# Two layers of cross attention: a lower place in the order for VectorE's transposes, and output products held back at the end

## The chip, the cores and the metric

The kernel runs on one core of one Trainium2 chip. The metric is the device time of one execution, in microseconds (us). A core has five engines that run their own instruction streams and wait for each other by semaphores: PE (TensorE, matrix products; its weight loads are listed apart as PEld), DVE (VectorE), ACT (ScalarE), POOL (GpSimd) and SP, which here only issues DMA transfers.

## The reference

Everything is float32: x is 8 x 100 x 512, the context 8 x 361 x 512. A first layer is a cross attention without heads. Then come two cross attentions with 16 heads of 128, and an MLP. Cut to what matters:

```python
def _cross_attention(q_in, kv_in, wq, bq, wk, bk, wv, bv, wo, bo, bias_k, bias_v):
    qh = (q_in @ wq + bq).reshape(b, q_len, H, K)          # H = 16, K = 128
    kh = (kv_in @ wk + bk).reshape(b, t, H, K)             # and one bias key
    vh = (kv_in @ wv + bv).reshape(b, t, H, K)             # and one bias value
    logits = jnp.einsum('bqhk,bthk->bhqt', qh, kh) / scale
    weights = jax.nn.softmax(logits, axis=-1)
    ctx = jnp.einsum('bhqt,bthk->bqhk', weights, vh).reshape(b, q_len, H * K)
    return ctx @ wo + bo
...
    x = x + alpha * (softmax(q k / sqrt(512)) v) @ w_o.T    # first layer, no heads
    x = x + _cross_attention(layer_norm(x), ctx, ...)       # twice, own weights
    x = x + gelu(layer_norm(x) @ w_fc1 + b_fc1) @ w_fc2 + b_fc2
```

## The kernel before, in words

**Steps.** The keys and values are never formed. Queries are multiplied by wq (pq, L623) and then by the head's key weights (pqw, L639, into the large buffer Z), and the scores are the product with the context itself. In the same way the softmax weights are first mixed with the context (into Z), and the value weights come after, in the output product. The eight batches go in four pairs (q = 0 to 3), and the 16 heads in three groups (g = 0, 1, 2) whose 100-row heads lie one after the other as 1600 rows: rows 0 to 576, 576 to 1088 and 1088 to 1600. So there are 24 steps (l, q, g) for the two layers l, and each has two halves j, one for each batch of the pair.

**One half.** Rows are taken in pairs of 128 (L692). A pair's scores are seven block products of a Strassen-Winograd scheme (PE L680/683, tiles sx, sy, sz), put together by copies on ACT (L708, L711, L714, L728) and additions on DVE (L718, L723, L724). The sums of blocks that it needs are made on POOL (L666 to L669), and POOL also writes the bias key's column (L717). Then: maximum on DVE (L736), exponential on ACT (L737), reciprocal (L313) and scaling (L314), and `turned` (L323), which turns the rows into columns by DVE transposes of 32 x 32 blocks (L329): four quarters of four instructions for a pair, written into the tile pT. When the last quarter of a group's last pair is done, `column_sums` (L752) sends the bias column to DRAM (L756, on SP's queue) and makes four sums on POOL (L757 to L760).

**Mix.** `mixed` (L784) multiplies pT with the context, again by a scheme of seven products, for two column halves m and in four parts each. Part 0 starts the tiles mx and mz (mz uses M1, which reads the result of L757); part 1 uses M2, which reads that of L759; part 2 makes M3 in mx and the tile my; part 3 makes A22 and A23 in the same PSUM bank as mx. Between part 2 and part 3 DVE has to read mx:

```python
            add(x, M3, 1)
            ...
            nc.vector.tensor_tensor(c22, x, c22, ALU.add)     # L819
            nc.vector.tensor_tensor(c11, y, c11, ALU.add)     # L820
        else:
            add(x, A22, 8, last=False)
```

L793 is the matmul in `add`; evictions go to ACT (L802, L805, L810, L824) and DVE (L813, L819, L820).

**Output.** `bias_probs` (L828) fetches the bias column's probabilities for a group, in two DMAs on SP's queue into the one buffer pb. `head_out` (L836) makes a head's output product: one POOL operation (L842), eight passes on PE (po, L845) against the weights wv, and one DVE operation (L852) into the tile oT. The weights wv come in a ring of two slots. `attn_out` (L863, pwo L869) is the product with wo for a batch pair, 128 passes, and `back` (L872) turns the result and adds it to x. The MLP consists of the norm's transposes (ph L540, then DVE L543), `hidden` (L883, pg L893) and `mlp_out` (L898, pf L905). L543 and ph are used for the query projections too.

**The order.** The program is a list of units. The main loop (from L1016) takes a half's score units in groups and lays the filling between them: the closing of the pair before (`close_units`), the projections of the next step (`ahead`), the mix of the half before, and, in halves j=1, the output products of the step before. `woven` spreads one list over another. `lead` is how many of the filling units come before the mix. After the loop comes `drain`: the last mix, output products and closing, with the MLP's norm between them. What the list says is not yet each engine's order: a scheduler takes instructions by priority, which is their place in the program, as they become ready by its own reckoning. `tc.high_priority(offset=-30)` around a block gives its instructions the priority of a place 30 later. Loads of weights go on SP's queue in the order of their use, as their ring's slots come free. P buffers (probabilities) are three, tiles of `sums` two, and all products share eight PSUM banks.

Of the kernel before, what the change touches and what calls it, by code (L numbers as in the profile page):

```python
# [16 lines left out]
B, L, S, D = 8, 100, 361, 512  # L17
# [5 lines left out]
QB = 2  # L23
# [10 lines left out]
WHOLE = ((0, 5), (5, 10), (10, 16))  # L34
# [8 lines left out]
A11, A12, A22, A13, A23, A33, M1, M2, M3, M4 = range(10)  # L43
LN_EPS = 1e-5
W_SLOTS, V_SLOTS, C_SLOTS, P_SLOTS = 6, 2, 2, 3
QD = 32


# [30 lines left out]
def two_cross_attentions(ctx: ExitStack, tc: tile.TileContext, a: dict, out: bass.AP):  # L79
    nc = tc.nc  # L80
# [11 lines left out]
    def psum(pool, shape, name):  # L92
        return pool.tile(shape, F32, tag=pool.name, name=name)
# [91 lines left out]
    units = []  # L185

    def unit(fn, *keys):
        return fn, keys
# [26 lines left out]
    for c in range(DT):  # L215
        rows = slice(c * P, (c + 1) * P)
# [106 lines left out]
    def turned(p, dst, tiles, rows, quarter):  # L323

        keys = slice(quarter * QD, (quarter + 1) * QD)
        src = p[:, :tiles, :].rearrange("p m (k j b) -> p m k j b", k=3, b=QD)
        dst = dst.rearrange("p k (m i a) -> p m k i a", m=tiles, a=QD)
        for i in range(rows // QD):
            nc.vector.transpose(dst[keys, :, :, i, :], src[i * QD : (i + 1) * QD, :, :, quarter, :])  # L329

    def ln_stats(b):
        st = small.tile([L, 6], F32, tag="stats", name=f"stats_{b}")
# [451 lines left out]
    def mixed(l, q, g, j, m, part):  # L784
        cx = rings["ctx"].tiles["ctx", l, q * QB + j].rearrange("p (m u n) -> p m u n", m=2, n=P)[:, m]
        pT = pTs[l, q, g, j]
        r0, r1 = ROWS[g]
        h = (r1 - r0) // 2
        c11, c12 = Z[:, 2 * m, j, r0 : r0 + h], Z[:, 2 * m, j, r0 + h : r1]
        c21, c22 = Z[:, 2 * m + 1, j, r0 : r0 + h], Z[:, 2 * m + 1, j, r0 + h : r1]  # L790

        def add(ps, blk, u, first=False, more=True, last=True, w=P):
            nc.tensor.matmul(  # L793
                ps, cx[:w, blk, :], pT[:w, u, :], start=first, stop=last, skip_group_check=more
            )

        name = f"{l}_{q}_{g}_{j}_{m}"
        if part == 0:
            x, z = psum(ps_mm, [P, h], f"mx_{name}"), psum(ps_mm, [P, h], f"mz_{name}")
            mixes[m] = x, z  # L800
            add(x, A11, 0, True, False)
            nc.scalar.copy(c11, x)  # L802
            add(z, M1, 6, True, False, False)
            add(z, A23, 5, more=False, w=TS)
            nc.scalar.copy(c22, z)  # L805
            return
        x, z = mixes[m]
        if part == 1:
            add(x, M2, 7)
            nc.scalar.copy(c12, x)  # L810
            add(z, M4, 3, last=False)
            add(z, A33, 5, w=TS)
            nc.vector.tensor_tensor(c12, z, c12, ALU.add)  # L813
        elif part == 2:
            add(x, M3, 1)
            y = psum(ps_mm, [P, h], f"my_{name}")
            add(y, A12, 2, True, False, False)
            add(y, A13, 4, more=False, w=TS)
# [4 lines that stand above are left out]
            add(x, A23, 4, w=TS)  # L823
            nc.scalar.copy(c21, x)  # L824
# [3 lines left out]
    def bias_probs(l, q, g):  # L828
        h0, h1 = WHOLE[g]
        t = work.tile([P, QB, 600], F32, tag="pb", name=f"pb_{l}_{q}_{g}", bufs=1)  # L830
        for j in range(QB):
            src = pbd[l, q * QB + j].rearrange("o r -> (o r)")[h0 * L : h1 * L]
            nc.sync.dma_start(out=t[:, j, : (h1 - h0) * L], in_=src.partition_broadcast(P))
        pbs[l, q] = t, h0

    def head_out(l, q, h):  # L836
        if (l, q) not in oTs:
            oTs[l, q] = opool.tile([P, H, NQ], F32, tag="o", name=f"oT_{l}_{q}")
        w = rings["v"].tiles["wv", l, q, h // 2].rearrange("p (c n) -> p c n", c=DT)
        t, h0 = pbs[l, q]  # L840
        add = t[:, :, (h - h0) * L : (h - h0 + 1) * L]
        nc.gpsimd.tensor_scalar(add, add, dv[:, l, h : h + 1], 1.0, ALU.mult, ALU.mult)  # L842
        ps = psum(ps_mm, [P, NQ], f"po_{l}_{q}_{h}")
        for c in range(DT):
            nc.tensor.matmul(  # L845
                ps,
                w[:, c, (h % 2) * K : (h % 2 + 1) * K],
                Z[:, c, :, h * L : (h + 1) * L],
                start=(c == 0),
                stop=(c == DT - 1),  # L850
            )
        nc.vector.scalar_tensor_tensor(  # L852
            oTs[l, q][:, h, :].rearrange("p (b t) -> p b t", b=QB),
            ps.rearrange("p (b t) -> p b t", b=QB),
            vec[f"bv{l + 1}"][:, h : h + 1],
            add,
            ALU.add,
            ALU.add,
        )
# [3 lines left out]
    def attn_out(l, q, c):  # L863
        if c == 0:
            ys[l, q] = work.tile([P, DT, NQ], F32, tag="y", name=f"y_{l}_{q}", bufs=1)
        ps = psum(ps_mm, [P, NQ], f"pwo_{l}_{q}_{c}")
        for h in range(H):
            w = w8(("wo", l, q, c, h // 8))
            nc.tensor.matmul(ps, w[:, h % 8, :], oTs[l, q][:, h, :], start=(h == 0), stop=(h == H - 1))  # L869
        nc.scalar.activation(ys[l, q][:, c, :], ps, AF.Identity, bias=vec_b[:, 6 + l, c : c + 1])  # L870
# [42 lines left out]
    steps = [(l, q, g) for l in range(2) for q in range(B // QB) for g in range(NG)]  # L913
# [27 lines left out]
    def mix_units(n, j):  # L941
        l, q, g = steps[n]
        return [
            unit(lambda m=m, part=part: mixed(l, q, g, j, m, part), ("ctx", ("ctx", l, q * QB + j)))
            for m in range(2)
            for part in range(4)
        ]

    def out_units(n):
        l, q, g = steps[n]  # L950
        return [unit(lambda h=h: head_out(l, q, h), ("v", ("wv", l, q, h // 2))) for h in range(*WHOLE[g])]

    def close_units(l, q):
        res = [
            unit(lambda c=c: attn_out(l, q, c), (W, ("wo", l, q, c, 0)), (W, ("wo", l, q, c, 1)))
            for c in range(DT)
        ]
        res += [unit(lambda j=j: back(ys[l, q], j * L, q * QB + j, ln_stats)) for j in range(QB)]
        return res
# [9 lines left out]

    def woven(x, y):  # L970

        res, k = [], 0
        for n, u in enumerate(x):
            res.append(u)
            upto = (n + 1) * len(y) // len(x)
            res += y[k:upto]
            k = upto
        return res
# [37 lines left out]
    for n, (l, q, g) in enumerate(steps):  # L1016
        ahead = project_units(n + 1) if n + 1 < len(steps) else []
        half_ahead = (len(ahead) + 1) // 2
        for j in range(QB):
            fill = []  # L1020
            if j == 0 and n and g == 1 and (l, q) != (0, 0):
                pl, pq, _ = steps[n - 2]
                fill += close_units(pl, pq)
            mix = mix_units(n, 0) if j else mix_units(n - 1, 1) if n else []
            part = ahead[:half_ahead] if j == 0 else ahead[half_ahead:]
            if j and n:
                outs = [unit(lambda n=n: bias_probs(*steps[n - 1]))] + out_units(n - 1)
                part = woven(part, outs) if len(part) > len(outs) else woven(outs, part)
            if mix:
                lead = (len(part) + 2) // 3  # L1030
                fill += part[:lead]
                part = part[lead:]
                fill += woven(part, mix) if len(part) > len(mix) else woven(mix, part)
            else:
                fill += part
            if l == 0 and q == 1:
                k = 2 * g + j
                fill += e_units(1)[4 * k // 3 : 4 * (k + 1) // 3]
            groups = score_units(n, j)
            k = 0  # L1040
            for i, us in enumerate(groups):
                units += us
                upto = (i + 1) * len(fill) // len(groups)
                units += fill[k:upto]
                k = upto
    n = len(steps) - 1
    drain = mix_units(n, 1) + [unit(lambda: bias_probs(*steps[n]))] + out_units(n)
    drain += close_units(1, B // QB - 1)
    norm, hid, mlp, end = mlp_units(0)
    norm1, hid1, mlp1, end1 = mlp_units(1)  # L1050
    units += woven(drain, norm)
    units += hid + woven(mlp, norm1) + woven(hid1, end) + mlp1 + end1
    emit()

# [24 lines left out]
```

## Time and profile before

| | |
|---|---|
| three runs, us | 2100.14, 2094.68, 2097.88 (median 2097.88) |
| the profiled execution, us | 2100.8 |
| its span, us | 2099.0 |
| its mean granted TensorE clock | 0.993 |
| PE idle within the span, us | 76.6 |
| memory traffic | 256.87 MB, mean 122 GB/s |

The profile is one execution. A line of a timeline gives the start, the length, the engine, the line of the kernel, the operation, what it writes and reads, how many instructions it groups, and in brackets how long the engine stood before it and what ended that. In the list of groups, the two numbers after the first bar are busy time in us and the mean of one instruction in ns. In a list of windows, each row gives the window's length, the busy time of PE, PEld, DVE, ACT and POOL (with the number of instructions), the granted clock of TensorE (1.00 is full), the busy share of the DMA engines and GB/s.

The 24 steps take most of the span, about 71 us each. The stretch from 1892 us on is the last output projection and the MLP.

### The profile page before, as it was taken

The page shows a single profiled execution, that of the slowest core. Times are in us where ns is not written, and L with a number is a line of the kernel's source. Part 1 is how long each engine was busy: PE and PEld are TensorE (multiplying, and loading weights), DVE is VectorE, ACT ScalarE, POOL GpSimd, SP SyncE. Part 2 cuts the span into 40 slices and gives each one's busy share as a digit, 9 for nine tenths or more (in the row PEclk, how much of TensorE's full clock was granted, in tenths as well). Part 3 has the DMA queues.
Part 4 walks back from the last instruction along what each step waited for, and adds up shares of the span by engine and source line. Part 5 has one row for each costly group of instructions (what it writes and reads, how often), then busy time and mean ns, then how long its engine had stood idle before and what let it go on. Part 6 is the DMA issues. An engine that isn't in the chain of part 4 may idle for free. (4 is left out here: it accounts for less than half of the span.)

```text
span 2099.0 us, 30154 instructions
## 1 busy us (share of the span) xinstructions
PE 2022.4 (96%) x10735; PEld 1774.3 (85%) x10735; DVE 1159.0 (55%) x3363; ACT 749.0 (36%) x1962; POOL 572.1 (27%) x1042
## 2 busy tenths in 40 slices
PE   9998999999999999999999999999999999989998
PEld 5768899898899898989898999899998998877555
DVE  2564776657764666466645665475647574661000
ACT  1224544424342444234423443344324442421110
POOL 3232442333242224223331323232322322310000
PEclk9999999999999999999999999999999999999999
DMA  8784325342544133414442344224332434113331
GB/s 251 260 293 136 96 76 182 119 147 79 158 128 140 61 122 119 150 36 141 155 140 82 106 131 131 84 86 143 108 110 81 151 95 120 51 53 121 100 102 50
DMA packets 254109, 256.87 MB, mean 122 GB/s; under 512 B 35756, under 2 KB 226640, under 8 KB 250632
## 3 DMA queue, kind: packets, MB, share of 16 engines
q1 hardware_dynamic: 249776, 244.58, 37.6%
q0 software_dynamic: 2112, 6.40, 0.9%
q10 hardware_dynamic: 2072, 3.97, 0.6%
q8 instruction: 85, 1.39, 0.3%
q14 instruction: 64, 0.52, 0.1%
HBM read 229.24 MB, written 25.67 MB: 121 GB/s over the span
## 5 line engine op out<-in xcount | busy, mean ns | idle before, releaser
L329 DVE STREAM_TRANSPOSE pT<-p 32x192 f32<-32x192 f32 (+1 forms) x1664 | 602.0, 362 | 85.4 <-ACT p L314 59.5
L793 PE MATMUL mx<-pT,ctx 128*128 128x256 f32 (+3 forms) x960 | 284.5, 395 | 32.7 <-DVE Z L819 28.6
L683 PE MATMUL sx<-cT,Z 128*128 128x181 f32 x1152 | 228.2, 317 | 5.0 <-DVE p L723 5.0
L793 PE MATMUL mz<-pT,ctx 105*128 105x256 f32 (+3 forms) x768 | 209.7, 395 | 13.9 <-POOL pT L757 12.3
L793 PEld LDWEIGHTS mx<-pT,ctx 128*128 128x128 f32 (+1 forms) x960 | 170.0, 190 | 55.7 <-DVE Z L819 31.2
L683 PEld LDWEIGHTS sx<-cT,Z 128*128 128x128 f32 x1152 | 195.2, 190 | 18.0 <-DVE p L723 6.5
L845 PE MATMUL po<-Z,wv 128*128 128x200 f32 x1024 | 199.0, 336 | 0.5 <-DMA wv<-in_L_xattn_wv_dram 0.5
L623 PE MATMUL pq<-hT,wq 128*128 128x200 f32 x1024 | 195.7, 335 | 3.9 <-DMA wq<-in_L_xattn_wq_dram 3.9
L639 PE MATMUL pqw<-q,wkT 128*128 128x200 f32 x1024 | 196.5, 334 | 0.0
L793 PEld LDWEIGHTS mz<-pT,ctx 128*128 128x128 f32 (+1 forms) x768 | 145.1, 192 | 49.6 <-POOL pT L757 16.3
L623 PEld LDWEIGHTS pq<-hT,wq 128*128 128x128 f32 x1024 | 176.6, 191 | 9.6 <-DMA wq<-in_L_xattn_wq_dram 4.1
L639 PEld LDWEIGHTS pqw<-q,wkT 128*128 128x128 f32 x1024 | 177.5, 191 | 5.4 <-issue 0.5
L845 PEld LDWEIGHTS po<-Z,wv 128*128 128x128 f32 x1024 | 176.5, 191 | 6.6 <-issue 1.6
L869 PE MATMUL pwo<-oT,wo 128*128 128x200 f32 x1024 | 176.0, 332 | 0.0
L869 PEld LDWEIGHTS pwo<-oT,wo 128*128 128x128 f32 x1024 | 173.3, 190 | 0.1
L737 ACT ACTIVATE p<-p,nm 128x362 f32<-128x362 f32 x192 | 114.8, 598 | 160.1 <-DVE nm L736 158.5
L666 POOL TENSOR_TENSOR sums<-Z 128x256 f32<-128x256 f32 x96 | 69.9, 728 | 348.7 <-ACT Z L642 194.1
L736 DVE TENSOR_REDUCE nm<-p 128x1 f32<-128x362 f32 x192 | 101.6, 529 | 98.2 <-ACT p L728 84.7
L642 ACT COPY Z<-pqw 128x400 f32<-128x400 f32 x256 | 122.9, 489 | 83.4 <-PE pqw L639 83.2
L683 PE MATMUL sz<-cT,sums 128*128 128x181 f32 x768 | 149.9, 317 | 0.0
L314 ACT ACTIVATE p<-p,rden 128x362 f32<-128x362 f32 (+2 forms) x216 | 129.6, 600 | 29.8 <-DVE rden L313 29.0
L683 PEld LDWEIGHTS sz<-cT,sums 128*128 128x128 f32 x768 | 124.5, 190 | 1.3 <-ACT p L711 1.3
(310 smaller groups left out, 2627.1 us busy)
## 6 DMA issues: line engine op xcount, KB each, us to landing
wv<-in_L_xattn_wv_dram SPq DMA_DIRECT2D x64, 512.0 KB
wq<-in_L_xattn_wq_dram SPq DMA_DIRECT2D x64, 512.0 KB
wo<-in_L_xattn_wo_dram SPq DMA_DIRECT2D x64, 512.0 KB
wkT<-wkd SPq DMA_DIRECT2D x48, 512.0 KB
cT<-cTd SPq DMA_DIRECT2D x16, 1267.0 KB
f<-in_L_xattn_w_fc_dram SPq DMA_DIRECT2D x32, 512.0 KB
wkr<-in_L_xattn_wk_dram SPq DMA_DIRECT2D x16, 512.0 KB
ctx<-cxd SPq DMA_DIRECT2D x16, 512.0 KB
```

What stands on the lines that cost most here:

```text
L314: nc.scalar.mul(p[:rows, :n], p[:rows, :n], rden[:rows])
L329: nc.vector.transpose(dst[keys, :, :, i, :], src[i * QD : (i + 1) * QD, :, :, quarter, :])
L623: nc.tensor.matmul(ps, w[:, c, (h % 2) * K : (h % 2 + 1) * K], hTs[l, q][:, c, :], start=(c == 0), stop=(c == DT - 1),)
L639: nc.tensor.matmul(ps[:, c, :], w[:, h % 2, cc * P : (cc + 1) * P], qs[h], start=True, stop=True)
L642: nc.scalar.copy(Z[:, 2 * c2 : 2 * c2 + 2, :, h * L : (h + 1) * L], ps.rearrange("p c (b t) -> p c b t", b=QB),)
L666: nc.gpsimd.tensor_tensor(t[:, 0], a2[:, :2, :], a2[:, 2:, :], ALU.add)
L683: nc.tensor.matmul(ps[:, :KH], st["a"][a][:, c, :], st["ct"][:, blk, c, :], start=(first and c == 0), stop=(c == 1), skip_group_check=not ...
L736: nc.vector.tensor_reduce(nm, p[:, :S1], AX.X, ALU.max, negate=True)
L737: nc.scalar.activation(p[:, :S1], p[:, :S1], AF.Exp, bias=nm, accum_out=den)
L793: nc.tensor.matmul(ps, cx[:w, blk, :], pT[:w, u, :], start=first, stop=last, skip_group_check=more)
L845: nc.tensor.matmul(ps, w[:, c, (h % 2) * K : (h % 2 + 1) * K], Z[:, c, :, h * L : (h + 1) * L], start=(c == 0), stop=(c == DT - 1),)
L869: nc.tensor.matmul(ps, w[:, h % 8, :], oTs[l, q][:, h, :], start=(h == 0), stop=(h == H - 1))
```

## The change

There are two parts.

First, the 16 transposes of a pair (and the eight of a first group's single tile of 64 rows) are issued with a priority 30 places later than where they stand. Nothing else about them changes.

Second, the output products are regrouped at the end. `out_units` now begins with the unit of `bias_probs`, which stood beside it before. In step 22 (the last but one), j=1, the output units of step 21 are not laid into the filling; they are put, with those of step 22, into `held`: twelve units, bias and heads 0 to 4, bias and heads 5 to 9. Step 23 takes six of them in its half j=0 and three (bias, heads 5 and 6) in j=1, where before it had those of step 22 in j=1. The last three (heads 7, 8, 9) come after the loop, followed by four of the eight transposes of the MLP's norm, and then the last mix and what follows it, with the other four. In step 23, `lead` is all but the last two of the filling units in j=0, and all but one in j=1. For all other steps the list of units stays as it was: `woven` now returns its second list when the first is empty, since a half with no output products passes through it too.

```diff
--- before.py
+++ after.py
@@ -43,6 +43,7 @@
 A11, A12, A22, A13, A23, A33, M1, M2, M3, M4 = range(10)
 LN_EPS = 1e-5
 W_SLOTS, V_SLOTS, C_SLOTS, P_SLOTS = 6, 2, 2, 3
+TURN_BEHIND = 30
 QD = 32
 
 
@@ -325,8 +326,9 @@
         keys = slice(quarter * QD, (quarter + 1) * QD)
         src = p[:, :tiles, :].rearrange("p m (k j b) -> p m k j b", k=3, b=QD)
         dst = dst.rearrange("p k (m i a) -> p m k i a", m=tiles, a=QD)
-        for i in range(rows // QD):
-            nc.vector.transpose(dst[keys, :, :, i, :], src[i * QD : (i + 1) * QD, :, :, quarter, :])
+        with tc.high_priority(offset=-TURN_BEHIND):
+            for i in range(rows // QD):
+                nc.vector.transpose(dst[keys, :, :, i, :], src[i * QD : (i + 1) * QD, :, :, quarter, :])
 
     def ln_stats(b):
         st = small.tile([L, 6], F32, tag="stats", name=f"stats_{b}")
@@ -948,7 +950,8 @@
 
     def out_units(n):
         l, q, g = steps[n]
-        return [unit(lambda h=h: head_out(l, q, h), ("v", ("wv", l, q, h // 2))) for h in range(*WHOLE[g])]
+        res = [unit(lambda h=h: head_out(l, q, h), ("v", ("wv", l, q, h // 2))) for h in range(*WHOLE[g])]
+        return [unit(lambda: bias_probs(l, q, g))] + res
 
     def close_units(l, q):
         res = [
@@ -969,6 +972,8 @@
 
     def woven(x, y):
 
+        if not x:
+            return y
         res, k = [], 0
         for n, u in enumerate(x):
             res.append(u)
@@ -1023,11 +1028,16 @@
                 fill += close_units(pl, pq)
             mix = mix_units(n, 0) if j else mix_units(n - 1, 1) if n else []
             part = ahead[:half_ahead] if j == 0 else ahead[half_ahead:]
-            if j and n:
-                outs = [unit(lambda n=n: bias_probs(*steps[n - 1]))] + out_units(n - 1)
-                part = woven(part, outs) if len(part) > len(outs) else woven(outs, part)
+            outs = []
+            if n == len(steps) - 1:
+                outs = held[:6] if j == 0 else held[6:9]
+            elif j and n:
+                outs = out_units(n - 1)
+                if n == len(steps) - 2:
+                    held, outs = outs + out_units(n), []
+            part = woven(part, outs) if len(part) > len(outs) else woven(outs, part)
             if mix:
-                lead = (len(part) + 2) // 3
+                lead = (len(part) + 2) // 3 if ahead else len(part) - 2 + j
                 fill += part[:lead]
                 part = part[lead:]
                 fill += woven(part, mix) if len(part) > len(mix) else woven(mix, part)
@@ -1044,11 +1054,10 @@
                 units += fill[k:upto]
                 k = upto
     n = len(steps) - 1
-    drain = mix_units(n, 1) + [unit(lambda: bias_probs(*steps[n]))] + out_units(n)
-    drain += close_units(1, B // QB - 1)
+    drain = mix_units(n, 1) + out_units(n) + close_units(1, B // QB - 1)
     norm, hid, mlp, end = mlp_units(0)
     norm1, hid1, mlp1, end1 = mlp_units(1)
-    units += woven(drain, norm)
+    units += held[9:] + norm[:4] + woven(drain, norm[4:])
     units += hid + woven(mlp, norm1) + woven(hid1, end) + mlp1 + end1
     emit()
 
```

The line numbers of the changed kernel are those of before plus one from L46 to L327, and plus two from L328 to L949: L819 becomes L821, L757 becomes L759.

## The prediction, made before the changed kernel was run

> **What bounds the kernel now.** I read the share of busy time first, then the engine's waits, then the timeline around the commonest wait, then ten-microsecond windows of the end.
>
> ```profile
> span 2099.0 us, 30154 instructions
> PE 2022.4 (96%) x10735; PEld 1774.3 (85%) x10735; DVE 1159.0 (55%) x3363; ACT 749.0 (36%) x1962; POOL 572.1 (27%) x1042
> ...
> L329 DVE STREAM_TRANSPOSE pT<-p 32x192 f32<-32x192 f32 (+1 forms) x1664 | 602.0, 362 | 85.4 <-ACT p L314 59.5
> ```
>
> PE is busy for all but 76.6 us of the span (2099.0 - 2022.4). The change adds no matmul, so it can win only from those 76.6 us and from time that PE is busy at a lower granted clock. The second engine, DVE, spends over half of its busy time in the transposes, 0.37 us each, in blocks of 16. PE's waits say what the 76.6 us are:
>
> ```profile
> engine line waited for: us in total, times, longest us
> PE mx L793 <- DVE Z L819: 28.6, 19, 2.1
> PE mz L793 <- POOL pT L757: 12.3, 8, 5.0
> PE sx L683 <- DVE p L723: 5.0, 3, 1.7
> PE pqk L350 <- DMA Z<-in_L_xattn_w_q_dram: 4.7, 1, 4.7
> PE sx L683 <- ACT p L708: 4.4, 5, 1.6
> ...
> PE mx L793 <- POOL pT L759: 2.7, 6, 0.5
> ```
>
> The first line is the largest. One of its places:
>
> ```profile
> 1560.81 6.11 DVE L329 STREAM_TRANSPOSE pT<-p 32x192 f32<-32x192 f32 x16 [0.66 <-ACT p L314]
> 1561.19 1.14 PE L793 MATMUL my<-pT,ctx 128*128 128x288 f32 x4
> 1566.96 0.46 DVE L819 TENSOR_TENSOR Z<-mx,Z 128x288 f32<-128x288 f32 x1
> 1567.01 0.73 POOL L757 TENSOR_TENSOR pT<-pT 128x256 f32<-128x256 f32 x1 [12.74 <-DVE pT L329]
> 1567.33 0.45 DVE L820 TENSOR_TENSOR Z<-my,Z 128x288 f32<-128x288 f32 x1
> 1567.47 1.24 PE L793 MATMUL mx<-pT,ctx 128*128 128x288 f32 x4 [1.88 <-DVE Z L819]
> ```
>
> The product M3 is in PSUM at about 1561.4, but DVE has 16 transposes ahead of the addition of L819, which starts at 1566.96. The last part of the mix writes the same PSUM bank as M3, so PE stands until L819 is done: 1.88 us. The transposes themselves have no such hurry here: the column sums they feed (L757 to L760) end near 1570, and the next mix reads them at 1573.58.
>
> The end of the attention has its own waits, all after 1790:
>
> ```profile
> 1817.20 1.13 PE L793 MATMUL mz<-pT,ctx 128*128 128x256 f32 x4 [1.99 <-POOL pT L757]
> 1831.52 0.88 PE L683 MATMUL sx<-cT,Z 128*128 128x181 f32 x4 [1.58 <-DVE p L723]
> 1842.46 1.13 PE L793 MATMUL mz<-pT,ctx 128*128 128x256 f32 x4 [2.37 <-POOL pT L757]
> 1869.88 2.08 PE L793 MATMUL mz<-pT,ctx 128*128 128x256 f32 x4 [4.97 <-POOL pT L757]
> ```
>
> No next step's projections are left there to fill PE, so the chain scores, softmax, transposes, column sums, mix stands open. After 1892 the output projection and MLP run without a gap.
>
> Some waits also cost afterwards: PE goes on at half clock for a while.
>
> ```profile
> 1783.00:1784.00 1.00, 1.00 (x4) 0.71 (x3) 0.00 (x0) 0.00 (x0) 0.92 (x3) 0.50 0.00 0
> 1860.00:1870.00 10.00, 5.03 (x27) 4.25 (x25) 8.12 (x22) 2.68 (x7) 0.81 (x2) 0.88 0.18 53
> ```
>
> The column after the engines is the granted clock: 0.50 after the 1.88 us wait at 1781.96. The same four matmuls took 2.02 us there and 1.24 us at 1567.47.
>
> **The skill.** "TensorE: Matmul & The Clock Gate", Part 1, says that TensorE falls to half clock after an idle window of about 3.4 us, that the window runs freely, and that this varies between runs. The trace agrees on the size of the drop (0.50, for some 3.4 us), not on the idle time: waits of 1.88 us already did it, though only at 911.4, 1351.7 and 1782.0 and not at 697, 1137 and 1567. "Perfetto Trace Analysis", GPSIMD and Tensor Engine sections, says that VectorE and GpSimd execute in strict order, which is what the 16 transposes ahead of L819 show. "VectorE: DVE Perf Modes", The three transpose paths, says the transpose works on 32x32 blocks; its price is for another type, so I use the trace's 0.37 us.
>
> **The change part by part.** The built program has the same number of instructions on every engine as before. Their static order tells what moved.
>
> *Transposes later, steps 0 to 21.* At places of the kind above (first head group, j=1, m=1), DVE had 16 transposes, L819, L820; it now has 3, L819, 2, L820, 11. At those of the third group (j=0, m=1) it had 15, L819, L820; it now has 5, L819, 2, L820, 4, L852, 4. L819 comes 10 to 13 transposes sooner, 3.7 to 4.8 us, against waits of 1.3 to 2.05 us. PE's own order changes too: the last mx part moves earlier at 13 places, ahead of an output product or other work that had covered part of DVE's delay. So the wait does not vanish by 3.7 us of slack: in the first group the part stands directly behind my, reached about 1562.2 in the example, and L819 would end about 1562.4; I leave 0.3 us at seven places, 2.1 us together, and none in the third group.
>
> Waits at the 13 places in the trace of before: 1.88, 1.89, 2.05, 1.88, 1.88, 1.88 (first group) and 1.88 (at 1083.88), six of 1.62 (third group): 13.3 + 9.7 = 23.1 us. Less 2.1: -21.0 us.
>
> What pays: the block's last transposes end later by what was put between them, 0.46 + 0.45 = 0.9 us in the first group, 1.25 with L852 in the third. The first has about 3.5 us of cover between the sums' end and the mix, the third at least 8: nothing. The second group's j=1 columns have none: at 1386.93 and its likes mz waits 0.3 us for L757 and mx then 0.54 for L759. One L543 (0.48 us) now precedes their last transpose: 6 places x 0.48 = 2.9 us. On POOL, L757 stands in most groups behind the pair of L717 (2 x 0.19 us). Where there is cover this is free, at those six places at most 2.3; I take 1.0, as L717 often waits for nothing. Sum of the body: -21.0 + 2.9 + 1.0 = about -17 us. Bounds: the additions nothing (-21), or twice what I take (-13).
>
> *Clock.* The drops at 911, 1352 and 1782 each cost half of 3.4 us, 1.7: 5.1 in all. Those waits go. The second group's waits become near 1.4 us together and could bring one drop back: -4 (bounds -5 and 0; a new wait of 1.9 would be as bad).
>
> *Held output products.* For step 22, bias and heads of steps 21 and 22 no longer stand before the last scores; six units go into step 23 j=0, three into j=1, heads 7 to 9 behind it with four transposes of the MLP's norm, then the last mix. Eight passes of L845 take 1.35 us, so some 13 us of PE work moves into or behind the open chain. But it is taken from before it: step 22 j=1 loses its filling, so its own waits, of some 0.2, open up. Stepping through PE, DVE, ACT and POOL in the new order with the durations of before, I get waits of 0.2, 1.3, 0.2, 0.5, 0.5, 1.4, 1.1, 0.5, 1.4, 0.5, 0.4, 4.1 and 0.55 (the wv load at 1888.73, moved with its ring of two slots): 12.6 us, where before has 1.99 + 1.58 + 0.28 + 2.37 + 4.97 + 0.55 = 11.7. The last wait stays, since its 16 transposes now share DVE with four L852 (1.7 us) while the held heads cover PE. Of the two half-clock stretches (1844 to 1847, 1867 to 1875, about 1.7 and 2.2 us) I expect one to go. +0.9 - 1.8: -1 us. Bounds: the steps lie on waits of a microsecond each, so -8 (the moved work covers the last two waits) to +5 (a late L757 behind L717, L667, L668 and L669 on POOL, 0.73 each for the last three, and another drop). On SP the bias loads and the wv loads come later with their heads, wo loads earlier; PE's pwo comes 20 us later, so nothing.
>
> Sum: -17 - 4 - 1 = -22 us. The profiled execution took 2100.8 us (span 2099.0 and 1.8 outside it): 2078.8. It stands 2.9 above the median of 2097.88, so on that scale 2076.
>
> **The rivals.** *Given back:* the wait on L819 goes, but PE, earlier by 1.9 us a step, meets the same DVE chain at the next use (scores at L723, columns at L757). For it: the waits on L723 and L708 already exist, 9.4 us. Against: DVE is at 55%, and the first and third groups have cover of microseconds. Half of the 22 stays: 2087 (2083 to 2095).
> *The end gains too:* held heads fill the 4.97 and 2.37 waits and both drops go: -8 instead of -1, and the additions in the body cost nothing (-4 more): 2065. For it: 13 us of PE work is moved there. Against: the step-through, in which DVE's 21.7 us in step 23 j=0 are the limit.
> *Column sums late (slower):* the transposes, 30 places lower, are overtaken by more than the order of the built program makes cheap: L757 on POOL waits behind L717, L667 to L669 for a score step that PE itself has put after the mix. Place: the mz that reads M1, 44 column sums in steps 0 to 21. It has to cost more than 23 + 6 us, so an average above 0.66 us of new wait at each of the 44; each long one may add 1.7 for the clock. At 0.9 us each with five drops: 40 + 8 - 23 = +25, less what the drops now cost (-5): about 2115. For it: L757 already makes the second line of the waits, and POOL holds four 0.73 us operations ahead. Against: 38 of the 44 have cover above the 0.9 to 1.3 us they get later.
> *Doesn't do what it says:* excluded, the static order shows the moved additions.
>
> **How the numbers follow.** Forecast 0.62 (2076, own range 2069 to 2084), given back 0.15, end too 0.10, late sums 0.13. The bound of what can be told is 0.3%, 6.3 us. Faster: 0.62 + 0.10 + two thirds of 0.15 = 0.82, take 0.81; same: 0.06; slower 0.13. The range 2063 to 2094 leaves out the slower case and edges of the others, about 0.18.
>
> **What would show it.** In the waits of the changed kernel: the line of L819 (now L821) falls from 28.6 to below 8 us with no place above 1.3 outside the end; L757 and L759 (L759, L761) grow by 3 to 5 us outside the end; PE's idle total falls to about 58 us; no clock of 0.8 in ten-microsecond windows around 911, 1352 and 1782. After 1790 the idle time stays near 12 us, with one wait of about 4 before the last mix. The prediction is wrong if L757's line grows past 25 us, if waits on L723 or L708 grow by the amount L819 loses, or if the end's idle falls below 5.

## The result, and the profile after

The changed kernel takes 2074.22 us (median of four runs, 2070.76 to 2074.61) against 2096.28 us before (median of four): a ratio of 0.9891, 95% interval 0.9869 to 0.9913. The profiled execution took 2074.07 us. Its page begins:

```profile
span 2072.3 us, 30186 instructions
...
PE 2014.7 (97%) x10735; PEld 1770.9 (85%) x10735; DVE 1165.6 (56%) x3363; ACT 748.5 (36%) x1962; POOL 575.7 (28%) x1042
```

PE idles 57.6 us (2072.3 - 2014.7) instead of 76.6, and is busy 7.7 us less with the same matmuls. Its waits (us in total, times, longest):

```profile
PE mz L795 <- POOL pT L759: 9.4, 7, 3.8
PE sx L685 <- ACT p L710: 6.7, 4, 3.1
PE mx L795 <- DVE Z L821: 5.5, 9, 1.9
PE mx L795 <- POOL pT L761: 5.2, 7, 1.4
...
PE sx L685 <- DVE p L725: 4.8, 5, 2.3
```

The line of L819 (now L821) falls from 28.6 to 5.5 us; the column sums' second line (L759, now L761) rises from 2.7 to 5.2. The timeline of the changed kernel at the place that the prediction took as its example:

```profile
1541.07 1.13 DVE L331 STREAM_TRANSPOSE pT<-p 32x192 f32<-32x192 f32 x3 [0.67 <-ACT p L315]
1541.45 1.14 PE L795 MATMUL my<-pT,ctx 128*128 128x288 f32 x4
1542.24 0.46 DVE L821 TENSOR_TENSOR Z<-mx,Z 128x288 f32<-128x288 f32 x1
1542.73 0.75 DVE L331 STREAM_TRANSPOSE pT<-p 32x192 f32<-32x192 f32 x2
1542.75 1.24 PE L795 MATMUL mx<-pT,ctx 128*128 128x288 f32 x4 [0.16 <-DVE Z L821]
1543.51 0.46 DVE L822 TENSOR_TENSOR Z<-my,Z 128x288 f32<-128x288 f32 x1
```

Three transposes instead of 16 stand ahead of the addition, and PE waits 0.16 us instead of 1.88. PE's own order changed with it, as predicted: the last part of mx now follows directly behind my, where before products of pqw, sx, sz and po stood between, which had covered some 3.4 us of DVE's delay. Now the place that pays, the second group's second half. First two lines of before, then the changed kernel:

```profile
1601.14 1.13 PE L793 MATMUL mz<-pT,ctx 128*128 128x256 f32 x4 [0.29 <-POOL pT L757]
1602.81 0.70 PE L793 MATMUL mx<-pT,ctx 128*128 128x256 f32 x2 [0.54 <-POOL pT L759]
```

```profile
1573.75 4.20 DVE L331 STREAM_TRANSPOSE pT<-p 32x192 f32<-32x192 f32 x11
1577.98 0.48 DVE L545 TENSOR_SCALAR hT<-ph,vec_b 128x200 f32<-128x200 f32 x1
1578.48 0.76 DVE L331 STREAM_TRANSPOSE pT<-p 32x192 f32<-32x192 f32 x2
1579.32 0.72 POOL L759 TENSOR_TENSOR pT<-pT 128x256 f32<-128x256 f32 x1 [0.91 <-DVE pT L331]
1580.10 1.13 PE L795 MATMUL mz<-pT,ctx 128*128 128x256 f32 x4 [0.82 <-POOL pT L759]
...
1582.15 0.70 PE L795 MATMUL mx<-pT,ctx 128*128 128x256 f32 x2 [0.92 <-POOL pT L761]
```

L545 (before: L543) has slipped in ahead of the last two transposes. The two waits are 0.82 and 0.92 us, where before they were 0.29 and 0.54, with one of 0.20 behind them (at 1604.01, on ACT).

To compare runs without the first part of the execution, which varies from run to run (the first mark below lies between 423.8 and 431.0 us in the traces of this study) and in which PE's idle time is nearly the same, 20.8 us before and 20.9 after, I take the first matmul of each of the eight `attn_out` (pwo) as a mark. "Steps" is the stretch from the first such mark to the next to last, "end" the one from there to the last. In before they are 428.79 to 1731.27 and 1731.27 to 1891.74. "Clock lost" is the length times one minus the granted clock, summed over windows of two microseconds; it counts also the half clock during which PE stands. A stretch of half clock lasts 3.4 us in these traces, or twice that, and so counts as 1.7 us or 3.4.

| | steps, us | PE idle | clock lost | end, us | PE idle | clock lost |
|---|---|---|---|---|---|---|
| before | 1302.5 | 35.5 | 3.4 | 160.5 | 13.7 | 6.8 |
| after | 1281.0 | 20.1 | 1.7 | 157.3 | 9.7 | 5.1 |

The steps give 21.5 us and the end 3.2. One interval without any half clock in either trace shows what a wait costs. The window views, before and then after (length, then busy time of PE, PEld, DVE, ACT and POOL, then the granted clock, here 1.00, DMA share and GB/s):

```profile
1516.79:1731.27 214.48, 209.53 (x1170) 194.23 (x1169) 130.97 (x366) 85.46 (x226) 64.03 (x118) 1.00 0.37 111
```

```profile
1497.05:1707.70 210.65, 208.55 (x1170) 194.35 (x1169) 131.28 (x366) 85.46 (x226) 64.42 (x118) 1.00 0.36 113
```

It is 3.83 us shorter, but only 2.85 of that is idle time (4.95 to 2.10). The other 0.98 is busy time for the same 1170 matmuls. The timeline shows six waits of 0.2 to 1.88 us in the first and three of 0.16 to 0.92 in the second, so some 0.3 us of busy time goes with each wait.

### The profile page after: what moved, and what is told of

The parts are those of the page before. It is cut to its first block, busy times and chain, and to the rows that moved or that the text cites. A ratio compares the mean times of both kernels' runs of the same rounds, so it can differ in the third digit from the quotient of the medians.

```text
span 2072.3 us, 30186 instructions
## 1 busy us (share of the span) xinstructions
PE 2014.7 (97%) x10735; PEld 1770.9 (85%) x10735; DVE 1165.6 (56%) x3363; ACT 748.5 (36%) x1962; POOL 575.7 (28%) x1042
## 5 line engine op out<-in xcount | busy, mean ns | idle before, releaser
L795 PE MATMUL mx<-pT,ctx 128*128 128x256 f32 (+3 forms) x960 | 282.7, 393 | 12.9 <-DVE Z L821 5.5
L847 PE MATMUL po<-Z,wv 128*128 128x200 f32 x1024 | 193.9, 333 | 0.6 <-DMA wv<-in_L_xattn_wv_dram 0.6
L719 POOL TENSOR_SCALAR p<-nsb 128x1 f32<-128x1 f32 x192 | 33.3, 193 | 526.3 <-DVE pT L331 481.8
```

Of the source, the lines that this page charges most:

```text
L795: nc.tensor.matmul(ps, cx[:w, blk, :], pT[:w, u, :], start=first, stop=last, skip_group_check=more)
L847: nc.tensor.matmul(ps, w[:, c, (h % 2) * K : (h % 2 + 1) * K], Z[:, c, :, h * L : (h + 1) * L], start=(c == 0), stop=(c == DT - 1),)
```

## The experiments

All ratios are to before, with 95% intervals, from five rounds each. They change only the order of the work.

**One part alone, twice.** The first run takes the transposes' priority alone:

```diff
+TURN_BEHIND = 30
...
+        with tc.high_priority(offset=-TURN_BEHIND):
+            for i in range(rows // QD):
+                nc.vector.transpose(dst[keys, :, :, i, :], src[i * QD : (i + 1) * QD, :, :, quarter, :])
```

> Only the transposes 30 places later; the output products of the last steps stay where they were before. Theory A (the gain is the wait on L819, at 13 places of the steps and the one near 1782; the held output products give nothing): 2074 to 2077 us, ratio to before 0.989 to 0.991; PE's line of waits for L819 near 6 us; the idle time behind 1760 near 12 us. Theory B (the held products give a third or more of the gain): 2081 to 2085 us, ratio 0.993 to 0.995.

The second takes all else of the change and leaves the transposes where they were:

```diff
-        with tc.high_priority(offset=-TURN_BEHIND):
-            for i in range(rows // QD):
-                nc.vector.transpose(dst[keys, :, :, i, :], src[i * QD : (i + 1) * QD, :, :, quarter, :])
+        for i in range(rows // QD):
+            nc.vector.transpose(dst[keys, :, :, i, :], src[i * QD : (i + 1) * QD, :, :, quarter, :])
```

> Only the output products held back; the transposes keep their priority. Theory A: 2095 to 2099 us, ratio 0.999 to 1.001, the wait on L819 at 28 us as before, and the idle time of the last steps moved from some places to others but not smaller than 11 us. Theory B: 2087 to 2091 us, ratio 0.995 to 0.997.

Measured: transposes alone 2076.69 us, 0.9903 (0.9883 to 0.9922); held products alone 2095.14 us, 0.9984 (0.9976 to 0.9993). Theory A holds for the first. For the second neither theory does: the time lies within A's range, but the ratio is below it and the idle time of the last steps below A's 11 us. The held products alone do gain, 0.16%, some 3 us, less than B asked. The trace shows a gain in the end, which is 156.4 us instead of 160.5, with 9.6 us of idle time instead of 13.7:

```profile
1731.04:1887.46 156.42, 146.81 (x778) 133.30 (x777) 90.84 (x251) 48.61 (x135) 40.85 (x74) 0.97 0.26 75
```

So I had the held products too small by themselves. Where the transposes are late, though, the end is 157.7 us without the held products and 157.3 with them. In these single executions the gain of 4 us shrinks to 0.5. A wait at the end of the changed kernel, in a timeline of DVE, POOL and PE, suggests a reason:

```profile
1838.86 1.51 DVE L331 STREAM_TRANSPOSE pT<-p 32x192 f32<-32x192 f32 x4
1840.38 0.42 DVE L854 SCALAR_TENSOR_TENSOR oT<-po,vecs,pb 128x200 f32<-128x200 f32 x1
1840.82 1.54 DVE L331 STREAM_TRANSPOSE pT<-p 32x192 f32<-32x192 f32 x4
1842.40 0.43 DVE L854 SCALAR_TENSOR_TENSOR oT<-po,vecs,pb 128x200 f32<-128x200 f32 x1
1842.86 0.75 DVE L331 STREAM_TRANSPOSE pT<-p 32x192 f32<-32x192 f32 x2
1843.75 0.72 POOL L759 TENSOR_TENSOR pT<-pT 128x256 f32<-128x256 f32 x1 [26.72 <-issue]
1844.52 2.08 PE L795 MATMUL mz<-pT,ctx 128*128 128x256 f32 x4 [3.84 <-POOL pT L759]
```

The evictions of the held products (L854) go between the last transposes, which everything waits for, and push back the mix. This is tested further down.

**Twenty places instead of thirty**, which is where the price of the second group should show:

```diff
-TURN_BEHIND = 30
+TURN_BEHIND = 20
```

> The changed kernel with the transposes 20 places later instead of 30. In its static order L819 comes as early as with 30, but no L543 stands before the last two transposes of the second group's second half. Theory A with this as the price (one L543 of 0.48 us at six places, 0.7 us of waits each with what follows): the waits for L757 and L759 at those six places fall back to 0.3 and 0.5 us, and the time to 2069 to 2071 us, ratio to before 0.987 to 0.988. Rival (the price comes from L717 ahead of L757 on POOL): those waits stay at 0.8 and 0.9, time 2073 to 2076 us.

Measured: 2068.19 us, 0.9859 (0.9838 to 0.9880), faster than expected. The same place in its trace:

```profile
1569.48 5.75 DVE L331 STREAM_TRANSPOSE pT<-p 32x192 f32<-32x192 f32 x15
1575.27 0.48 DVE L545 TENSOR_SCALAR hT<-ph,vec_b 128x200 f32<-128x200 f32 x1
1575.32 0.73 POOL L759 TENSOR_TENSOR pT<-pT 128x256 f32<-128x256 f32 x1 [0.41 <-DVE pT L331]
1576.10 1.13 PE L795 MATMUL mz<-pT,ctx 128*128 128x256 f32 x4 [0.32 <-POOL pT L759]
...
1577.58 0.70 PE L795 MATMUL mx<-pT,ctx 128*128 128x256 f32 x2 [0.35 <-POOL pT L761]
```

All transposes come first, L545 follows, and the waits are 0.32, 0.35 and 0.38 us (the last one on ACT). In the steps idle time falls from 20.1 to 15.6 us, and 4.1 of these 4.5 us are the waits of the second group's second halves: L545 was the price of the 30 places there. The rival (L717 on POOL) is out; in the changed kernel POOL had stood idle for 0.91 us before L759, waiting for the transposes. The end is 2.1 us shorter too (155.2), with one half clock less.

**The addition sooner instead of the transposes later.** If only L819 counts, it is enough to move that. The transposes go back to their own priority, and the held products stay:

```diff
-            nc.vector.tensor_tensor(c22, x, c22, ALU.add)
+            with tc.high_priority(offset=30):
+                nc.vector.tensor_tensor(c22, x, c22, ALU.add)
```

> The output products held back as in the changed kernel; the transposes keep their priority, and only the addition of L819 is issued 30 places earlier in priority. In its static order L819 has 3 (first group) or 6 (third group) transposes before it instead of 16. Theory A (what counts is L819 alone): waits for L819 near 6 us, those for L757 and L759 at the second group as before (0.3 and 0.5), 2068 to 2071 us, ratio 0.986 to 0.988. Rival C (the later transposes also help otherwise, since other DVE work comes sooner): 2077 us or more, ratio 0.991 or more, with waits on L723 or on output products in place of those on L819.

Measured: 2074.87 us, 0.9888 (0.9867 to 0.9909), between the two. Theory A's time is missed. The waits of this kernel say why:

```profile
PE mx L794 <- DVE Z L821: 8.2, 12, 2.0
...
PE po L847 <- DVE Z L822: 5.3, 5, 1.4
```

The second line is new. L820 (here L822), left behind the rest of the transposes, frees the PSUM bank of my late, and now an output product waits for that bank. So the change works through both additions, and my argument had named one. With both raised:

```diff
-            nc.vector.tensor_tensor(c22, x, c22, ALU.add)
-            nc.vector.tensor_tensor(c11, y, c11, ALU.add)
+            with tc.high_priority(offset=30):
+                nc.vector.tensor_tensor(c22, x, c22, ALU.add)
+                nc.vector.tensor_tensor(c11, y, c11, ALU.add)
```

> Output products held back; transposes keep their priority; the additions of L819 and of L820 are both issued 30 places earlier in priority. Theory (both additions hold up PE, L819 the bank of mx and L820 the bank of my, which an output product takes next; where the transposes stand otherwise doesn't matter): the line of output products that wait for L820 (5.3 us where L819 alone was raised) goes to below 1 us, the waits for the column sums stay as before the change, the last steps gain some 7 us as with L819 alone, and the time is 2065 to 2069 us, ratio 0.984 to 0.987. Rival (the transposes' delay itself is needed): 2073 us or more.

Measured: 2067.83 us, 0.9852 (0.9828 to 0.9876). The wait for L822 is no longer among this kernel's longest lines, the steps take 1278.6 us (1281.0 in the changed kernel) and the end 153.8. The transposes' own delay is not needed; the place of the two additions is enough, beside the held products.

**The end.** Where the additions were raised, the end took 153.3 and 153.8 us, where the transposes were late everywhere 155 to 158. To test whether it is the late transposes that cost there, steps 22 and 23 got their own priority back, with 30 and with 20 places elsewhere (`turned` takes the offset as a further argument):

```diff
-        turned(p, columns(l, q, g, j)[:, :, c0 : c0 + n], len(dens), rows, quarter)
+        turned(p, columns(l, q, g, j)[:, :, c0 : c0 + n], len(dens), rows, quarter,
+               0 if (l, q) == (1, 3) and g else TURN_BEHIND)
```

> The changed kernel (30 places), with the transposes of steps 22 and 23 at their own priority. Theory (in the last two steps nothing covers a later transpose, so there the lower priority costs what the held output products bring): the stretch from the first product with wo before the last one to the last gains 6 to 7 us on before where the changed kernel gains 3.2, time 2069 to 2072 us, ratio 0.986 to 0.988. Rival (the held products bring nothing once the transposes are late in the other steps): 2073 to 2076 us, the stretch 3 us.

> As the run before, with 20 places instead of 30. Theory: the gains add, 4 us in the steps (no L543 ahead of the second group's last transposes) and 2 us in the last ones against 20 places everywhere (2068.2 us): 2065 to 2067 us, ratio 0.984 to 0.986. Rival: the last steps don't depend on the priority, 2068 us.

Measured: 2074.53 us, 0.9885 (0.9864 to 0.9907), and 2069.69 us, 0.9859 (0.9835 to 0.9884). The ends came out at 156.6 and 156.7 us: the expectation was missed twice. The timeline of PE in the first of the two shows that the edit had taken back one place too many:

```profile
1758.76 1.24 PE L796 MATMUL mx<-pT,ctx 128*128 128x288 f32 x4 [1.85 <-DVE Z L822]
```

The transposes that stand ahead of this L819 (here L822) belong to step 22's first half. The wait of 1.85 us is back, and a half clock after it. So only step 22's second half and step 23 were left out:

```diff
-               0 if (l, q) == (1, 3) and g else TURN_BEHIND)
+               0 if (l, q) == (1, 3) and g + j > 1 else TURN_BEHIND)
```

> The changed kernel (30 places), with the transposes at their own priority in step 22's second half and in step 23 only, so that those which stand ahead of L819 near 1755 us are late again. Theory (the last steps pay for late transposes; the run that left all of steps 22 and 23 out lost that again to one wait of 1.85 us for L819 and its half clock): the stretch from the next to last close to the last, 160.5 us before and 157.3 in the changed kernel, is 153 to 154 us, as where the additions were raised (153.3 and 153.8); time 2069 to 2073 us, ratio 0.986 to 0.988. Rival: it stays at 156 to 157 us, and the gain of the raised additions there has another reason.

> The same with 20 places. Theory: the two savings add: the steps as with 20 places everywhere, the last stretch 153 to 154 us (155.2 with 20 everywhere): 2064 to 2068 us, ratio 0.983 to 0.986. Rival: 2068 to 2070 us, no better than 20 places everywhere.

Measured: with 30 places 2073.88 us, 0.9876 (0.9854 to 0.9897), above its expected time, though within the expected ratio; with 20 places 2066.87 us, 0.9850 (0.9827 to 0.9873). The end is 153.5 and 153.7 us, as expected:

```profile
1704.32:1857.98 153.66, 145.60 (x779) 132.06 (x777) 90.73 (x251) 48.70 (x135) 40.93 (x74) 0.98 0.26 76
```

The last wait of the mix, 3.84 us in the changed kernel, is now 1.48 us with 30 places and 2.07 with 20:

```profile
1836.97 1.22 PE L796 MATMUL mx<-pT,ctx 128*128 128x256 f32 x2 [2.07 <-DVE oT L855]
```

So late transposes do cost something in the last step and a half: 3.7 us in the end at 30 places (157.3 to 153.5) and 1.5 at 20 (155.2 to 153.7). Of the 3.7 us, 1.3 are idle time and 1.7 one stretch of half clock, which need not come back in another execution. That this cost hides the held products' gain in the changed kernel is shown only in part. They take 4.1 us of idle time from the end alone (13.7 to 9.6) and 3.2 beside late transposes (12.9 to 9.7); of the 3.5 us between the two gains only 0.9 are idle time, and 1.7 are one stretch of half clock. The total times don't show it: 0.16% alone, and 0.9903 against 0.9891 beside late transposes, whose intervals overlap. A kernel with the last steps left out and no held products was not run.

The two kernels with 30 places don't differ measurably in their total times. In the steps their instructions stand in the same order on PE, DVE, ACT and POOL, yet the profiled execution of the one with the last steps left out lost 5.1 us of clock there against 1.7.

| | ratio | steps, us | PE idle | clock lost | end, us | PE idle | clock lost |
|---|---|---|---|---|---|---|---|
| transposes alone | 0.9903 | 1281.0 | 20.2 | 1.7 | 157.7 | 12.9 | 5.1 |
| held products alone | 0.9984 | 1304.9 | 34.5 | 6.8 | 156.4 | 9.6 | 5.1 |
| 20 places | 0.9859 | 1278.2 | 15.6 | 1.7 | 155.2 | 9.1 | 3.4 |
| L819 raised | 0.9888 | 1283.7 | 21.3 | 0.0 | 153.3 | 8.5 | 3.4 |
| both raised | 0.9852 | 1278.6 | 17.6 | 0.0 | 153.8 | 8.4 | 3.4 |
| 30, steps 22 and 23 out | 0.9885 | 1280.8 | 19.9 | 1.7 | 156.6 | 11.1 | 3.4 |
| 20, steps 22 and 23 out | 0.9859 | 1277.2 | 16.1 | 0.0 | 156.7 | 11.1 | 3.4 |
| 30, last step and a half out | 0.9876 | 1284.1 | 20.1 | 5.1 | 153.5 | 8.4 | 3.4 |
| 20, last step and a half out | 0.9850 | 1277.2 | 16.2 | 0.0 | 153.7 | 8.1 | 3.4 |

The last row has the lowest ratio of the study. It is faster than the kernel before; against the changed kernel (0.9891, 0.9869 to 0.9913) the intervals just touch. Twenty places everywhere and both additions raised are as fast within their intervals.

## Why the prediction was right

The prediction said 2076 us; 2074.22 was measured. Point by point:

- *The waits on L819, -21.0 us.* Right: 28.6 to 5.5 us is -23.1, with a residue of 0.16 to 0.17 us at five places and 0.26 at a sixth, where I had left 0.3. What remains stands mostly at three other places, and one of them is 1.92 us (at 372.41), above the 1.3 us that I gave as a limit. That the second addition matters as well was missing from the argument; it made no difference to the sum, since the change moves both.
- *The second group, +2.9 and +1.0.* Right in size, and the part with L543 shown by the run with 20 places, where these waits together fall back to 0.5 us above before. Place by place it is uneven: 0.7 us more at three places, 1.9 at one (near 940), 0.3 at two and nothing at one, together 4.6. The part with L717 has no support: POOL waits for DVE there.
- *The clock, -4.* This term was mis-sized. The three drops are gone, as I said, but two came back, at 372 and 941, and I had allowed for one. The second of them comes with two column-sum waits of 1.03 and 1.38 us. Up to 1735 us both traces lose 3.4 us to the clock (from 180 us on); the end loses 1.7 less.
- *A term that I left out* came in its place: each wait that goes also takes busy time with it. In the steps the stretch is 21.5 us shorter, of which 15.4 are idle time and 1.7 clock; 4.4 remain. Waits of over 0.15 us fall from 32 to 23 there; at some 0.3 us each, nine of them make 2.7, and where the other 1.7 us come from stays open. The errors in the two terms are of similar size and cancel. That is luck, and the total is better than its terms.
- *The held products, -1.* Near in its sum, and by luck. The end is 3.2 us shorter, but the wait near 1782 (1.88 to 0.17 us) and its half clock, 1.7 us each, had been counted in the terms above; so about nothing is left for this one. Inside it, idle time fell by 2.3 us where I had a rise of 0.9, and no half clock went where I had one go for 1.8. PE is busy 0.8 us longer in the end although a half clock is gone; two transposes of the norm moved into it, and there are ten waits instead of seven. The held products alone do better, as their own run shows. My range for this term, -8 to +5, held both. The last wait was put at 4.1 us and is 3.84, with four evictions among the last transposes, as predicted.
- *The rivals.* Nothing was given back at L723 (5.0 to 4.8 us); L708 rose from 4.4 to 6.7 by one wait of 3.1 us at 207.68, before the first mark. The late sums did not come to 0.66 us at 44 places, only to 0.3 to 1.9 us at six.

The profiled executions differ by 26.7 us and the medians by 22.1. Some 2.5 us of this were there at the first step's first score product (181.1 us before, 178.6 after), ahead of the steps.

## What to carry to other kernels

When an engine that works in strict order holds a long block without haste ahead of an operation that frees another engine's buffer, the gain is the sum of those waits plus what each wait costs beside its idle time. Name every operation in the block's way that frees a buffer, not only the first. Here it did equally well to bring the two additions forward (0.9852) and to push the block back by only 20 places (0.9859). Pushing it back by 30 did less (0.9891): a block that is pushed back also falls behind whatever else becomes ready, and where it ends a chain without cover (here the second group's half and the last steps) that shows at once. An edit that gains little beside another may be hidden by it in part: run each alone, and compare stretch by stretch, idle time apart from clock.

## What the runs showed that was not expected

A wait of PE costs more than its idle time: some 0.3 us of busy time for each (0.98 us for three waits less, at full clock in both). Part of it can be seen in the timeline: four products of 288 columns take 1.24 us right behind a wait (1542.75 above) and 1.14 without one (1541.45). And half clock can follow quite short waits. The Trainium skill, "TensorE: Matmul & The Clock Gate", section "Why this matters for your kernels", warns of idle gaps above about 3 us. Here a wait of 1.92 us at 372.41 and the pair of 1.03 and 1.38 us within 3.6 us at 940 were enough (granted clock, the number before the DMA share, in windows of the changed kernel):

```profile
370.00:380.00 10.00, 8.08 (x36) 7.54 (x35) 7.78 (x22) 5.06 (x13) 2.19 (x4) 0.83 0.39 112
940.00:950.00 10.00, 9.80 (x46) 8.06 (x47) 5.27 (x15) 4.46 (x12) 4.26 (x9) 0.83 0.09 2
```

Each such drop is 1.7 us of clock. The page's figure and these waits differ, and the waits decide: here shorter gaps than 3 us were enough. But not every such wait is followed by a drop: in the same execution one of 1.61 us at 549.94 and the pairs of 0.82 and 0.92 us near 728, 1371 and 1582 were not. The same page, Part 1, says that the window runs freely and that this varies by run. That agrees: the steps lost between 0 and 6.8 us of clock in the kernels above, and two kernels with the same order there (30 places, with and without the last step and a half) lost 1.7 and 5.1. Up to the next to last mark, with the stretch before the first one, it is 5.1 and 10.2. So differences of up to some 5 us between single executions of this kernel can be the clock's alone.
